# Seven products for eight in the second layer's attention, with the next sample normed twice

## The chip, the cores and the metric

The kernel runs on one core of a Trainium2 chip. The metric is the device time of one execution in microseconds, the median of several runs. A core has a matrix engine (TensorE, in the profile PE, with its weight loads as PEld), a vector engine (VectorE, DVE), an engine for functions such as the exponential (ScalarE, ACT), a general one (GpSimd, POOL), and one that issues transfers (SyncE, SP). They work side by side and wait for each other at semaphores. Each takes its own instructions in the order in which the program lists them. Results of TensorE go to PSUM, which the kernel uses in pairs of banks, a bank being 128 x 512 numbers of 32 bits; everything else stands in SBUF.

## The reference

Two attention blocks follow each other on 8 samples of 512 channels x 1024 positions, all in float32. Layer 0 has 8 heads, layer 1 has one head over all 512 channels. The change is in layer 1 and in what stands just before and after it.

```python
# layer 1; x is what layer 0 gave
n = (x - mean) * rsqrt(var + EPS) * gn_gamma + gn_beta      # mean and var of the whole sample
nf = n.reshape(b, c, h * w)                                 # c = 512, h * w = 1024
q = einsum('oc,bcs->bos', wq, nf) + bq
k = einsum('oc,bcs->bos', wk, nf) + bk
v = einsum('oc,bcs->bos', wv, nf) + bv
attn = softmax(einsum('bci,bcj->bij', q, k) * c ** (-0.5), axis=-1)
out = einsum('bcj,bij->bci', v, attn)
out = einsum('oc,bcs->bos', wo, out) + bo
return x + out
```

The kernel multiplies wq with wk, and wv with wo, once at its start. So a sample's keys in layer 1 are the normed input itself (`hs`), and the values already carry the output projection.

## The kernel before: the parts that the change touches

A product of two 2 x 2 block matrices takes eight block products, or seven with some sums and differences ahead of and behind them (one step of Strassen's recursion, in Winograd's form). The kernel already makes q, k, v and the projections this way:

```python
def strassen(multiply, done, name):          # A: blocks A11.. and S1..S4; B: blocks B11.. and T1..T4
    ...
    p1, p2 = two("o", 0, ("A11", "B11"), ("A12", "B21"))   # a pair of PSUM banks of tag "o"
    u1 = tile_u(f"u1_{name}")
    nc.scalar.copy(u1, p1)
    done(0, 0, p2, u1)
    yield                                                  # step 0
    o = banks("s", f"ps_{name}_1")                         # a pair of tag "s"
    p5, p6 = o[:, 0, :], o[:, 1, :]
    multiply(p5, "S1", "T1")
    yield                                                  # step 1
    multiply(p6, "S2", "T2")
    u2 = plus(p6, u1, "u2")                                # plus: one tensor_tensor on VectorE
    u4 = plus(p5, u2, "u4")
    yield                                                  # step 2
    p7, p4 = two("o", 2, ("S3", "T3"), ("A22", "T4"))
    u3 = plus(p7, u2, "u3")
    done(1, 1, p5, u3)
    done(1, 0, p4, u3)
    yield                                                  # step 3
    p3, _ = two("s", 3, ("S4", "B22"))
    done(0, 1, p3, u4)
    yield                                                  # step 4
```

`in_turn` runs such groups one after the other, `together` takes a step of each in turn, and `at_steps(groups, {n: [hook]})` writes other instructions into the program after step n. PSUM has two pairs of banks for each of the tags "s" and "o". The pool `t` holds 34 tiles of 128 x 1024, the pool `u` 5 of 128 x 512. The order on TensorE, VectorE and ScalarE is that of the Python text.

Layer 1's attention works on halves g of the queries, with plain products:

```python
def attention1(xs, hs, bs, b):
    ...                                    # q and v by strassen, from bs (hs and its T1..T4)
    def scores(g, kt2):                    # 2 x 128 keys x 512 queries
        s = banks("s", f"s_{name}")
        for j in range(2):
            kt = 2 * kt2 + j
            for cc in range(NC):           # NC = 4 chunks of 128 channels
                nc.tensor.matmul(s[:, j, :], piece(hs, cc, kt // 4)[...], qs[cc][:, g, :],
                                 start=cc == 0, stop=cc == NC - 1)
        ...
        p = exponentials(s, C**-0.5, accs.get(g), first, name)  # ACT: Exp of 128 x 1024; DVE: acc += p

    def values(g, ps):
        for oc2 in range(NC // 2):
            o = banks("o", f"ps_o_1_{b}_{oc2}_{g}")
            for j in range(2):
                oc = 2 * oc2 + j
                for kt in range(NT):       # NT = 8 tiles of 128 keys
                    nc.tensor.matmul(o[:, j, :], vs[kt][:, oc * P : (oc + 1) * P], ps[kt // 2][:, kt % 2, :], ...)
                if oc == 0:
                    t = banks("o", f"ps_sum_1_{b}_{g}")[:, 0, :]
                    for i in range(2):     # the sum of the exponentials over all keys
                        nc.tensor.matmul(t, ones, accs[g][:, i, :], start=i == 0, stop=i == 1)
                    inv = one_over(t, f"1_{b}_{g}")
                    held(inv, f"inv_1_{b}_{g}")
            for j in range(2):
                ...
                nc.vector.tensor_tensor(t, o[:, j, :], inv, ALU.mult)
                nc.vector.scalar_tensor_tensor(x, t, made["bias1"][:, oc : oc + 1], x, ALU.add, ALU.add)

    ps0 = [scores(0, kt2) for kt2 in range(NT // 2)]
    ps1 = [scores(1, 0)]
    values(0, ps0)
    ps1 += [scores(1, kt2) for kt2 in range(1, NT // 2)]
    values(1, ps1)
```

`one_over` lets ScalarE read the sums (`held`, for a check of their size) and then takes their reciprocal on VectorE. What surrounds it:

```python
# layer0(b): the second half of q and k of sample b; meanwhile sample b + 1 is normed, and its T1..T4 are made
hooks = {8: [lambda: score(0), lambda: score(1)]}         # first scores of layer 0
...
hooks[3] = [lambda: norm_next().normed(norm_next().xs)]
hooks[5] = [lambda: combine.first(norm_next().xs)]
hooks[7] = [combine.second]
...
at_steps(in_turn(*pairs_qk(w, 1, bs, qs, ks, b)), hooks)

# the loop over samples, after layer 0 of sample b: the first half of q and k of sample b + 1,
# from the 4 tiles of its normed x and its 4 tiles T1..T4, which are then kept for layer 0 of b + 1
at_steps(
    in_turn(*pairs_qk(next_weight(), 0, bs, qs, ks, b + 1)),
    {n + 1: [step] for n, step in enumerate(steps)},      # mean, variance, normed, T1 T2, T3 T4 of layer 1
)
...
attention1(xs, hs, combine.parts, b)
```

Of the kernel before, what the change touches and what calls it, by code (L numbers as in the profile page):

```python
# [31 lines left out]
FP = mybir.dt.float32  # L32
AF = mybir.ActivationFunctionType
ALU = mybir.AluOpType
# [6 lines left out]
P = 128  # L41
# [18 lines left out]
def two_attention_blocks(  # L60
# [32 lines left out]
    def tile2(name):  # L93
        return tpool.tile([P, 2, HALF], FP, tag="t", name=name)
# [241 lines left out]
    class Combined:  # L336


        def __init__(self, name):
            self.parts = {f"T{i}": tile2(f"t{i}_{name}") for i in range(1, 5)}  # L340

        def first(self, quarters):
            (b11, b12), (b21, b22) = quarters
            self.parts.update(B11=b11, B21=b21, B22=b22)
            nc.vector.tensor_tensor(self.parts["T1"], b12, b11, ALU.subtract)  # L345
            nc.vector.tensor_tensor(self.parts["T2"], b22, self.parts["T1"], ALU.subtract)
            self.b12 = b12
# [9 lines left out]
        c.second()  # L357
        return c.parts

    def strassen(multiply, done, name):  # L360

        def two(tag, n, *parts):
            o = banks(tag, f"ps_{name}_{n}")
            for i, (a, b) in enumerate(parts):
                multiply(o[:, i, :], a, b)
            return o[:, 0, :], o[:, 1, :]

        def plus(bank, u, what):
            t = tile_u(f"{what}_{name}")
            nc.vector.tensor_tensor(t, bank, u, ALU.add)  # L373
            return t

        p1, p2 = two("o", 0, ("A11", "B11"), ("A12", "B21"))
# [3 lines that stand above are left out]
        yield  # L380
        o = banks("s", f"ps_{name}_1")
        p5, p6 = o[:, 0, :], o[:, 1, :]
        multiply(p5, "S1", "T1")
        yield
        multiply(p6, "S2", "T2")
        u2 = plus(p6, u1, "u2")
        u4 = plus(p5, u2, "u4")
        yield
        p7, p4 = two("o", 2, ("S3", "T3"), ("A22", "T4"))
        u3 = plus(p7, u2, "u3")  # L390
        done(1, 1, p5, u3)
        done(1, 0, p4, u3)
        yield
        p3, _ = two("s", 3, ("S4", "B22"))
        done(0, 1, p3, u4)
        yield

# [14 lines left out]
    def at_steps(steps, hooks):  # L412

        n = -1
        for n, _ in enumerate(steps):
            for hook in hooks.get(n, []):
                hook()
        assert n >= max(hooks, default=-1)

    def by_channels(w, c, bs):  # L420


        def multiply(bank, a, b):
            for k in range(2):
                nc.tensor.matmul(  # L425
                    bank, w[a][:, k, c * P : (c + 1) * P], bs[b][:, k, :],
                    start=k == 0, stop=k == 1,
                )

        return multiply  # L430
# [12 lines left out]

        return multiply

    def make_channels(w, c, oc, bs, bias, to, name):

        def done(i, half, bank, u):  # L450
            n = oc + 2 * i
            nc.vector.scalar_tensor_tensor(  # L452
                to(n, half), bank, bias[:, n : n + 1], u, ALU.add, ALU.add
            )

        return strassen(by_channels(w, c, bs), done, f"{name}_{oc}")

    def make_v(w, n2, bs, vs, name):

# [75 lines left out]
    def blank(n, name):  # L535
        return [tile2(f"{name}_{i}") for i in range(n)]
# [3 lines left out]

    def pairs_qk(w, oc, bs, qs, ks, b):

        for ts, n, bias, name in [(qs, 0, V_BQ0, "q"), (ks, 1, V_BK0, "k")]:
            for i in (oc, oc + 2):
                ts[i] = tile2(f"{name}_0_{b}_{i}")
            yield make_channels(
                w.parts[n], 0, oc, bs, vec[:, bias : bias + NC],
                lambda chunk, half, ts=ts: ts[chunk][:, half, :], f"{name}_0_{b}",
            )

    ORDER = [0, 2, 1, 3]
# [1 line left out]
    def layer0(bs, qs, ks, b, load_next, norm_next):  # L553
# [72 lines left out]
        def score(i):  # L626
            ps[i] = scores(*units[i])

        w = next_weight()
        if b == 0:  # L630
            w.finish()
            waiting[0].finish()
            made["bias0"] = bias_through(square_of_parts(waiting[0]), V_BV0, V_BP0, "bias0")
        hooks = {8: [lambda: score(0), lambda: score(1)]}
        if norm_next is not None:
            hooks[0] = [lambda: norm_next().mean_of_all()]
            hooks[2] = [lambda: norm_next().variance_of_all()]
# [63 lines left out]
            held(invs.pop(at), f"inv_0_{b}_{at[0]}_{at[1]}")  # L701
        return xs, norm, bs_next

    def attention1(xs, hs, bs, b):

        qs = blank(NC, f"q_1_{b}")
        w = next_weight().parts[0]
        at_steps(in_turn(*[
            make_channels(
                w, c, c, bs, made["bias_q1"], lambda chunk, half: qs[chunk][:, half, :], f"q_1_{b}"  # L710
            )
            for c in range(2)
        ]), {})
        vs = blank(NT // 2, f"v_1_{b}")
        w = next_weight().parts[0]
        at_steps(in_turn(*[make_v(w, n2, bs, vs, f"v_1_{b}") for n2 in range(2)]), {})
        vs = [vs[nt // 2][:, nt % 2, :] for nt in range(NT)]
        accs = {}

        def scores(g, kt2):  # L720
            name = f"1_{b}_{g}_{kt2}"
            s = banks("s", f"s_{name}")
            for j in range(2):
                kt = 2 * kt2 + j
                for cc in range(NC):
                    nc.tensor.matmul(  # L726
                        s[:, j, :], piece(hs, cc, kt // 4)[:, kt % 4 * P : (kt % 4 + 1) * P],
                        qs[cc][:, g, :], start=cc == 0, stop=cc == NC - 1,
                    )
            if kt2 == 1:  # L730
                first, accs[g] = accs[g], accpool.tile(
                    [P, 2, HALF], FP, tag="acc", name=f"acc_{name}"
                )
            else:
                first = accs.get(g)
            p = exponentials(s, C**-0.5, accs.get(g), first, name)
            if kt2 == 0:
                accs[g] = p
            return p

        def values(g, ps):
            for oc2 in range(NC // 2):
                o = banks("o", f"ps_o_1_{b}_{oc2}_{g}")
                for j in range(2):
                    oc = 2 * oc2 + j
                    for kt in range(NT):
                        nc.tensor.matmul(  # L747
                            o[:, j, :], vs[kt][:, oc * P : (oc + 1) * P], ps[kt // 2][:, kt % 2, :],
                            start=kt == 0, stop=kt == NT - 1,
                        )  # L750
                    if oc == 0:
                        t = banks("o", f"ps_sum_1_{b}_{g}")[:, 0, :]
                        for i in range(2):
                            nc.tensor.matmul(t, ones, accs[g][:, i, :], start=i == 0, stop=i == 1)  # L754
                        inv = one_over(t, f"1_{b}_{g}")
                        held(inv, f"inv_1_{b}_{g}")
                for j in range(2):
                    oc = 2 * oc2 + j
                    t, x = tile_u(f"o_1_{b}_{oc}_{g}"), piece(xs, oc, g)
                    nc.vector.tensor_tensor(t, o[:, j, :], inv, ALU.mult)  # L760
                    nc.vector.scalar_tensor_tensor(
                        x, t, made["bias1"][:, oc : oc + 1], x, ALU.add, ALU.add
                    )

        ps0 = [scores(0, kt2) for kt2 in range(NT // 2)]
        ps1 = [scores(1, 0)]
        values(0, ps0)
        ps1 += [scores(1, kt2) for kt2 in range(1, NT // 2)]
        values(1, ps1)

    made = {}

# [1 line left out]
    with tc.manual_schedule(engines={PE, ACT, DVE}):  # L774
# [15 lines left out]
        for b in range(B):  # L790
            ahead = []

            def load_next():
                ahead.append(norm0(load_x(b + 1, nc.sync), b + 1))

            norm_next = (lambda: ahead[0]) if b + 1 < B else None
            xs, norm, bs = layer0(bs, qs, ks, b, load_next, norm_next)

            qs, ks = [None] * NC, [None] * NC
            hs, combine = quarters_of(f"h_1_{b}"), Combined(f"1_{b}")  # L800
            steps = [
                norm.mean_of_all, norm.variance_of_all, lambda: norm.normed(hs),
                lambda: combine.first(hs), combine.second,
            ]
            if b + 1 < B:
                at_steps(
                    in_turn(*pairs_qk(next_weight(), 0, bs, qs, ks, b + 1)),
                    {n + 1: [step] for n, step in enumerate(steps)},
                )
            else:  # L810
                for step in steps:
                    step()
            attention1(xs, hs, combine.parts, b)
            for half in range(2):
                for i in range(2):
                    nc.sync.dma_start(quarter_of(out, b, i, half), xs[i][half])
# [404 lines left out]
```

## Time and profile before

| | |
|---|---|
| median of 3 runs | 3153.16 us (3148.82 to 3154.3) |
| span of the profiled execution | 3153.6 us, mean granted TensorE clock 0.994 |
| from the scores of sample 1 to those of sample 2 in layer 1 | 745.81 to 1128.76 us, so 382.95 us a sample |
| layer 1's scores and values of sample 1 | 745.81 to 859.19 us, 113.4 us |
| HBM traffic | 48 GB/s over the span |

A line of instruction groups gives the source line, engine, operation, tiles written and read, shapes and number, then busy time, the mean ns of one, and the idle time ahead of it with what ended it. A float32 matmul leaves two records on PE, so the counts of matmuls there are twice those of the program. The end of a PE record is modelled and laps over the next, so the time of a matmul is read from the distance between starts. A timeline line gives the start, the length, and the merged instructions from there on.

### The profile page before, as it was taken

The page shows a single profiled execution, that of the slowest core. Times are in us where ns is not written, and L with a number is a line of the kernel's source. Part 1 is how long each engine was busy: PE and PEld are TensorE (multiplying, and loading weights), DVE is VectorE, ACT ScalarE, POOL GpSimd, SP SyncE. Part 2 cuts the span into 40 slices and gives each one's busy share as a digit, 9 for nine tenths or more (in the row PEclk, how much of TensorE's full clock was granted, in tenths as well). Part 3 has the DMA queues.
Part 4 walks back from the last instruction along what each step waited for, and adds up shares of the span by engine and source line. Part 5 has one row for each costly group of instructions (what it writes and reads, how often), then busy time and mean ns, then how long its engine had stood idle before and what let it go on. Part 6 is the DMA issues. An engine that isn't in the chain of part 4 may idle for free.

```text
span 3153.6 us, 33267 instructions
## 1 busy us (share of the span) xinstructions
PE 3091.7 (98%) x14370; PEld 1435.4 (46%) x14370; DVE 1808.9 (57%) x2130; ACT 835.8 (27%) x1125; POOL 13.9 (0%) x26
## 2 busy tenths in 40 slices
PE   7999999999999999999999999999999999999898
PEld 4533545335443455334553354533545335453353
DVE  4588226882278723786237852489425883248822
ACT  0162002620036100460005500154011630116200
POOL 0000000000000000000000000000000000000000
PEclk9999999999999999999999999999999999999999
DMA  6300112011120111201011011100211001020000
GB/s 230 144 1 24 70 47 81 1 47 47 54 74 1 47 47 54 74 1 70 30 70 51 1 70 63 64 24 11 83 40 64 24 24 70 14 87 1 1 0 28
DMA packets 42314, 152.70 MB, mean 48 GB/s; under 512 B 2992, under 2 KB 9136, under 8 KB 35760
## 3 DMA queue, kind: packets, MB, share of 16 engines
q1 hardware_dynamic: 38208, 146.29, 12.9%
q10 hardware_dynamic: 3952, 4.22, 0.4%
q8 instruction: 114, 1.87, 0.2%
q14 instruction: 40, 0.33, 0.0%
HBM read 122.71 MB, written 27.79 MB: 48 GB/s over the span
## 4 chain that ended last, share of the span: by engine, by line
PE 93%; DVE 6%; issue 1%; DMA 0%; ACT 0%; POOL 0%; DVEq 0%; POOLq 0%; ACTq 0%
PE s L726 14%; PE ps_o L747 14%; PE s L581 14%; PE ps_o L602 14%; PE ps_v L439 12%; PE ps_q L425 11%; PE ps_k L425 5%; PE ps_p L425 4%; PE ps_sum L616 2%; DVE p L684 1%; DVE x L687 1%; PE ps_sum L754 1%; DVE part L287 1%; PE ps_wvo L507 1%; DVE u_k L373 0%
## 5 line engine op out<-in xcount | busy, mean ns | idle before, releaser
L518 ACT ACTIVATE p<-s 128x1024 f32<-128x1024 f32 x576 | 590.3, 1025 | 922.8 <-PE s L726 581.3
L520 DVE TENSOR_TENSOR acc<-acc,p 128x1024 f32<-128x1024 f32 x416 | 508.9, 1223 | 269.0 <-ACT p L518 255.3
L581 PE MATMUL s<-q,k 64*64 64x512 f32 x4096 | 535.6, 593 | 7.2 <-DVE k L452 7.2
L602 PE MATMUL ps_o<-p,v 64*64 64x512 f32 x4096 | 528.7, 589 | 0.0
L747 PE MATMUL ps_o<-p,v 128*128 128x512 f32 x1024 | 444.7, 592 | 0.0
L726 PE MATMUL s<-q,h 128*128 128x512 f32 x1024 | 442.7, 593 | 0.0
L532 DVE RECIPROCAL inv<-ps_sum 128x512 f32<-128x512 f32 x80 | 268.4, 3356 | 183.8 <-ACT held_sum L527 183.8
L747 PEld LDWEIGHTS ps_o<-p,v 128*128 128x128 f32 x1024 | 194.6, 190 | 244.9 <-issue 244.9
L726 PEld LDWEIGHTS s<-q,h 128*128 128x128 f32 x1024 | 193.9, 190 | 243.1 <-issue 243.1
L581 PEld LDWEIGHTS s<-q,k 64*64 64x64 f32 x4096 | 148.8, 133 | 310.5 <-issue 223.6
L602 PEld LDWEIGHTS ps_o<-p,v 64*64 64x64 f32 x4096 | 156.6, 133 | 282.8 <-issue 270.9
L520 DVE TENSOR_TENSOR acc<-p,p 128x1024 f32<-128x1024 f32 x80 | 98.0, 1225 | 195.7 <-ACT p L518 195.7
L760 DVE TENSOR_TENSOR o<-ps_o,inv 128x512 f32<-128x512 f32 x64 | 44.0, 687 | 218.0 <-PE ps_o L747 218.0
L378 ACT COPY u_v<-ps_v 128x512 f32<-128x512 f32 x32 | 18.8, 586 | 421.4 <-PE ps_v L439 421.4
L373 DVE TENSOR_TENSOR u_v<-ps_v,u_v 128x512 f32<-128x512 f32 x96 | 66.3, 691 | 110.0 <-PE ps_v L439 108.9
L378 ACT COPY u_q<-ps_q 128x512 f32<-128x512 f32 x32 | 18.8, 586 | 415.2 <-PE ps_q L425 415.2
L466 DVE TENSOR_TENSOR v<-ps_v,u_v 128x512 f32<-128x512 f32 x128 | 82.8, 684 | 79.7 <-ACT u_v L378 78.6
L373 DVE TENSOR_TENSOR u_q<-ps_q,u_q 128x512 f32<-128x512 f32 x96 | 66.4, 692 | 95.5 <-PE ps_q L425 94.4
L425 PE MATMUL ps_q<-t,w_qk 128*128 128x512 f32 x256 | 118.0, 602 | 2.1 <-DVE t L345 2.1
L439 PE MATMUL ps_v<-w_v,t 128*128 128x256 f32 x512 | 113.1, 379 | 0.0
L439 PE MATMUL ps_v<-w_wvo,t 128*128 128x256 f32 x512 | 113.1, 379 | 0.0
L425 PE MATMUL ps_q<-t,w_wqk 128*128 128x512 f32 x256 | 112.5, 592 | 0.0
(138 smaller groups left out, 2628.1 us busy)
## 6 DMA issues: line engine op xcount, KB each, us to landing
x<-in_x SPq DMA_DIRECT2D x60, 512.0 KB, 8.7
w_qk<-stored_qk SPq DMA_DIRECT2D x14, 1792.0 KB, 7.3
out<-x SPq DMA_DIRECT2D x32, 512.0 KB, 2.8
w_wqk<-stored_wqk SPq DMA_DIRECT2D x8, 1792.0 KB, 7.2
w_wvo<-stored_wvo SPq DMA_DIRECT2D x8, 1792.0 KB, 7.3
w_v<-stored_v SPq DMA_DIRECT2D x7, 1792.0 KB, 7.2
w_p<-stored_p SPq DMA_DIRECT2D x7, 1792.0 KB, 7.2
stored_qk<-w_qk SPq DMA_DIRECT2D x2, 1792.0 KB, 7.1
```

Source lines behind the costliest of these rows:

```text
L373: nc.vector.tensor_tensor(t, bank, u, ALU.add)
L425: nc.tensor.matmul(bank, w[a][:, k, c * P : (c + 1) * P], bs[b][:, k, :], start=k == 0, stop=k == 1,)
L439: nc.tensor.matmul(bank[:, u * 2 * P : (u + 1) * 2 * P], bs[b][:, k, n * P : (n + 1) * P], w[a][:, k, :], start=k == 0, stop=k == 1,)
L466: nc.vector.tensor_tensor(v, pairs(bank), pairs(u), ALU.add)
L518: nc.scalar.activation(p, s, AF.Exp, scale=factor)
L520: nc.vector.tensor_tensor(acc, first, p, ALU.add)
L532: nc.vector.reciprocal(inv, ps)
L581: nc.tensor.matmul(s[cols, j, :], flat(ks[pair])[rows, k0 : k0 + HD], qs[pair][rows, g, :], start=True, stop=True,)
L602: nc.tensor.matmul(o[cols, half, :], vs[kt][rows, c0 : c0 + HD], p[rows, j, :], start=kt == 0, stop=kt == NT - 1,)
L616: nc.tensor.matmul(ps[j * HD : (j + 1) * HD, :], ones[:, :HD], accs[pair, g][:, j, :], start=True, stop=True,)
L726: nc.tensor.matmul(s[:, j, :], piece(hs, cc, kt // 4)[:, kt % 4 * P : (kt % 4 + 1) * P], qs[cc][:, g, :], start=cc == 0, stop=cc == NC - 1,)
L747: nc.tensor.matmul(o[:, j, :], vs[kt][:, oc * P : (oc + 1) * P], ps[kt // 2][:, kt % 2, :], start=kt == 0, stop=kt == NT - 1,)
```

## The change

In layer 1 the scores and the product with V also become block products of seven. The queries' quarters get S1 to S4 (`finish_q`), and the normed input already has T1 to T4, from the making of q and v. For the product with V the sums are made of the values (S1 to S4) and of the exponentials (T1 to T4), since a block product of exponentials needs differences of whole blocks. All scores of a sample therefore come first. The softmax's sums of all queries are then taken with two matmuls where there were four. Keeping all exponentials and their differences needs more of the 34 tiles; to free them, the next sample's normed input and T1 to T4 are thrown away after their use for half of q and k. While the values are computed, x is loaded again, normed again with the scale and shift that are still there, and combined again. Three smaller things move: the last product of layer 0's k goes to an "o" pair of banks, the second score of layer 0 stands behind it, and layer 1's mean and the steps after it stand one step later.

```diff
-            self.parts = {f"T{i}": tile2(f"t{i}_{name}") for i in range(1, 5)}
+            self.name, self.parts = name, {}
         def first(self, quarters):
             (b11, b12), (b21, b22) = quarters
+            for i in range(1, 5):
+                self.parts[f"T{i}"] = tile2(f"t{i}_{self.name}")
...
-        p3, _ = two("s", 3, ("S4", "B22"))
+        p3, _ = two(last, 3, ("S4", "B22"))          # last is "o" for k of oc = 1, else "s"
...
-        hooks = {8: [lambda: score(0), lambda: score(1)]}
+        hooks = {8: [lambda: score(0)], 9: [lambda: score(1)]}
...
+        def finish_q():
+            for i in range(1, 5):
+                q_parts[f"S{i}"] = tile2(f"s{i}_q_{b}")
+            finish(q_parts, a21)
+        at_steps(in_turn(*[make_v(w, n2, bs, vs, f"v_1_{b}") for n2 in range(2)]), {1: [finish_q]})
...
+        def scores(t):
+            def multiply(bank, a, b):
+                for k in range(2):
                     nc.tensor.matmul(
+                        bank, bs[b][:, k, t * P : (t + 1) * P], q_parts[a][:, k, :],
+                        start=k == 0, stop=k == 1,
                     )
+            def done(i, j, bank, u):
+                p = ps[j][t // 2][i][:, t % 2, :]
+                nc.vector.tensor_tensor(p, bank, u, ALU.add)
+                nc.scalar.activation(p, p, AF.Exp, scale=C**-0.5)
+                if late:
+                    add_up(*late.pop())              # acc += the exponentials of one done() before
+                late.append((i, p))
+            return strassen(multiply, done, f"s_1_{b}_{t}")
+        at_steps(in_turn(*[scores(t) for t in range(NT // 2)]), {})
...
+        def finish_values(n):                        # S_n of the values, T_n of the exponentials
+            for k in range(2):
+                ...
+                nc.vector.tensor_tensor(a[f"S{n}"], x, y, op)                    # 128 x 512
+                ...
+                nc.vector.tensor_tensor(b[f"T{n}"], x, y, ALU.subtract)          # 128 x 1024
+        def sums():
+            t = banks("s", f"ps_sum_1_{b}")
+            for i in range(2):
+                nc.tensor.matmul(t[:, i, :], ones, acc[:, i, :], start=True, stop=True)
+            for i in range(2):
+                invs.append(one_over(t[:, i, :], f"1_{b}_{i}"))
+        def values(c):
+            def multiply(bank, a, b):
+                for kt in range(NT // 2):
+                    nc.tensor.matmul(bank, v_parts[kt // 2][a][...], p_parts[kt // 2][b][:, kt % 2, :], ...)
+            def done(i, j, bank, u):
+                if not invs:
+                    sums()
+                ...
+                nc.vector.tensor_tensor(t, bank, u, ALU.add)
+                nc.vector.tensor_tensor(t, t, invs[j], ALU.mult)
+                nc.vector.scalar_tensor_tensor(
+                    x, t, made["bias1"][:, chunk : chunk + 1], x, ALU.add, ALU.add
+                )
+            return strassen(multiply, done, f"o_1_{b}_{c}")
+        finish_values(1)
+        hooks = {1: [lambda: finish_values(2)], 3: [lambda: finish_values(3)], 5: [lambda: finish_values(4)]}
+        ...                                          # and at_values, below
+        at_steps(together(values(0), values(1)), hooks)
...
-                    {n + 1: [step] for n, step in enumerate(steps)},
+                    {n + 2: [step] for n, step in enumerate(steps)},
...
+                at_values = {
+                    2: [load_again], 6: [lambda: again.normed(again.xs)],
+                    8: [lambda: combine_next.first(again.xs)], 9: [combine_next.second],
+                }
+                bs = combine_next.parts
```

## The prediction

> **What bounds the kernel now.** I read the shares of the engines first, then what TensorE waited for, then the costliest groups, then one sample of layer 1 in order of time.
>
> ```profile
> PE 3091.7 (98%) x14370; PEld 1435.4 (46%) x14370; DVE 1808.9 (57%) x2130; ACT 835.8 (27%) x1125; POOL 13.9 (0%) x26
> ```
>
> PE is busy for 98% of the span, so only 62 us of 3154 are without a matmul. What TensorE waited for (us in total, times, longest):
>
> ```profile
> PE ps_m L268 <- DVE stat L290: 13.3, 8, 6.2
> PE ps_wvo L507 <- DMA wo<-in_w_o: 11.2, 1, 11.2
> PE ps_p L425 <- DVE p L684: 10.9, 8, 1.4
> PE s L581 <- DVE k L452: 7.2, 8, 1.0
> ```
>
> Each is one short wait a sample, or the start. So a matmul taken away shortens the span by its whole length, as long as what feeds and empties it keeps up. The groups concerned:
>
> ```profile
> L520 DVE TENSOR_TENSOR acc<-acc,p 128x1024 f32<-128x1024 f32 x416 | 508.9, 1223 | 269.0 <-ACT p L518 255.3
> L747 PE MATMUL ps_o<-p,v 128*128 128x512 f32 x1024 | 444.7, 592 | 0.0
> L726 PE MATMUL s<-q,h 128*128 128x512 f32 x1024 | 442.7, 593 | 0.0
> L760 DVE TENSOR_TENSOR o<-ps_o,inv 128x512 f32<-128x512 f32 x64 | 44.0, 687 | 218.0 <-PE ps_o L747 218.0
> ```
>
> Scores (L726) and values (L747) have 1024 records each, so 512 matmuls, 64 a sample; neither waits for anything. The mean of 592 ns laps over the next record. The distance between starts gives the true time (timeline of PE, sample 1):
>
> ```profile
> 745.81 34.57 PE L726 MATMUL s<-q,h 128*128 128x512 f32 x80
> 780.22 7.03 PE L747 MATMUL ps_o<-p,v 128*128 128x512 f32 x16
> 787.09 1.88 PE L754 MATMUL ps_sum<-acc,ones 128*128 128x512 f32 x4
> 788.80 20.76 PE L747 MATMUL ps_o<-p,v 128*128 128x512 f32 x48
> ```
>
> 80 records are 40 matmuls, and 780.22 - 745.81 = 34.41 us, so 0.860 us each. Four records of the sums are two matmuls in 1.71 us. The whole stretch has 132 matmuls in 113.4 us (0.859). How the other engines stood in four stretches (length, then busy us of PE, PEld, DVE, ACT, POOL, clock, DMA): scores, values with sums, v of layer 1, and the end of layer 0's projection.
>
> ```profile
> 745.90:780.40 34.50, 34.50 (x82) 15.37 (x82) 4.64 (x5) 4.10 (x4) 0.00 (x0) 1.00 0.15 54
> 780.40:809.50 29.10, 29.10 (x69) 12.84 (x69) 6.15 (x5) 2.44 (x5) 0.00 (x0) 1.00 0.05 19
> 721.70:745.90 24.20, 24.20 (x114) 21.11 (x113) 9.52 (x15) 1.17 (x2) 0.00 (x0) 1.00 0.21 76
> 1027.70:1054.80 27.10, 25.74 (x65) 10.74 (x62) 24.41 (x31) 3.17 (x7) 0.00 (x0) 1.00 0.00 1
> ```
>
> Layer 1's attention leaves VectorE nearly free. The third row is a Strassen stage made `in_turn`: TensorE has no gap. The fourth is one made `together` with VectorE 90% busy: it cost TensorE 1.36 us. These two are my models for the new scores and the new values.
>
> **What the Trainium skill says.** "FP8 and Floating Point Precision", TensorE Precision Notes: true FP32 takes 4 passes through the array. "TensorE: Matmul & The Clock Gate", What's actually happening, gives the array 2.4 GHz; an estimate from both is 4 x 512 / 2.4 = 853 ns a matmul, and the trace shows 860. So the time lies in the columns streamed, and block products of the same shape cost the same. "VectorE: DVE Perf Modes", The TRN2 errata: an fp32 tensor_tensor of N columns takes (N + 151) / 0.96 ns, so 691 and 1224; the trace has 692 (u_q) and 1223 (L520). "PSUM — Partial Sum Buffer", PSUM bank collisions: two engines may not touch one bank at once, so the program has to order them. The trace agrees: the reciprocal (L532, 3356 ns) follows ScalarE's read of the sum.
>
> **TensorE's part.** Scores: 4 groups x 7 products x 2 matmuls = 56 a sample, not 64. Values: 2 x 7 x 4 = 56, not 64. Sums: 2, not 4. That is 18 fewer, all 128 x 512: 18 x 0.861 = 15.5 us a sample, 124.0 us in 8. I count all of it, because none of the removed matmuls hid a wait.
>
> **The small moves.** The mean of layer 1 one step later: PE's wait for L290 was 13.3 us in 8, of which 6.2 in the last sample, where there is no q and k to put it behind and nothing changes. The other 7.1 us should go. First scores of layer 0: the wait of 7.2 us was for k to leave the "s" banks; with a product between the two scores and another pair of banks it should go too. At the very end, three VectorE steps follow the last product in place of four (2.8 us from 3143.47): 0.7 us, once.
>
> **VectorE in the scores.** Per sample 12 sums u, 16 sums in `done` and 14 additions to acc, 42 x 0.69 = 29.0 us, beside 56 x 0.861 = 48.2 us of TensorE. ScalarE: 16 exponentials of 128 x 512 at about 0.6 (held_inv of that shape took 625 ns) and 4 copies of 0.59, 12 us. With 60% load and the same banks as in the stage for v I expect no wait. An addition to acc stands one `done` behind its exponential, so it finds it done. The four sums of `finish_q` (4 x 1.22 = 4.9 us) fall into v's 24 us, where VectorE had 9.5: no wait.
>
> **VectorE in the values: the tight place.** `finish_values` 8 x (0.69 + 1.22) = 15.3; reciprocals 2 x 3.36 = 6.7; u 6 x 0.69 = 4.1; `done` 8 x (0.69 + 0.69 + 0.75) = 17.0; norming again 4 x 0.54 = 2.2; T1 to T4 again 4 x 1.22 = 4.9. Sum 50.2 us, beside 58 x 0.861 = 49.9 of TensorE. It is as full as the projection. So I laid both orders side by side, with 0 at the first product of values:
>
> - TensorE: p1 and p2 of the first half to 6.9, the two sums to 8.6, p1 and p2 of the second to 15.5, p5 twice to 22.4, p6 twice to 29.3, p7 and p4 of the first to 36.2, of the second to 43.0, p3 twice to 49.9.
> - VectorE: last additions to acc to 2.2, S1 and T1 to 6.0, reciprocals (first sum 7.8, ScalarE's read to 8.6) to 15.4, two `done` to 19.9, S2 and T2 to 23.7, S3 and T3 to 27.5, u2 and u4 twice to 30.8, S4 and T4 to 34.6, then u3 and two `done` of the first half to 39.5, norming to 41.7, those of the second to 46.6, the last `done` and T1 to T4 to about 56.
>
> Where they meet: T2's first half is needed at 22.4 and ready at 21.9; its second at 24.1 and 23.7; T4's first half at 32.7 and 32.7; its second at 34.5 and 34.6. So p6 just passes and p4 may wait some tenths. Later VectorE is behind, but p3 needs only the bank of p5, free at 43.1, while TensorE comes there at 46.8. The next sample's v then runs its first two products from the normed x, needs T1 at 53 (ready 50) and T4 near 59 (ready 56). I put the waits at 0.5 us a sample, 4 us in all.
>
> **The second load.** 2 MB more for seven samples, against 48 GB/s over the span. In the order of transfers these loads stand behind the store of the first quarter of x, which is ready at about 20; their tiles were set free earlier, at the end of the scores. The listing of transfers has 8.7 us from issue to landing for x, so they land near 31, and norming comes at 39.5. Hidden.
>
> **The sum.** 3153.2 - 124.0 - 7.1 - 7.2 - 0.7 + 4 = 3018 us, 4.3% less.
>
> **Rivals.** First, VectorE becomes the bound in the values. For it: 50.2 against 49.9, and a chain of sums, reciprocals and differences with no slack at p4. The projection with the same fill lost 1.36 us. Against it: independent VectorE instructions follow each other faster than their length (L661 to L662 in the projection start 0.60 us apart at 0.68 us each). If it bites, it makes 2 to 4 us a sample: 3030 to 3046. Second, the reload is late: it shares the transfers with the weights, and one store holds back four loads. Then norming holds VectorE, the banks of p5 stay taken, and p3 waits. It has some 8 us to spare before norming waits and some 3 more before TensorE does; past that it may cost 5 us a sample, near 3055. Third, a chain in the scores: bank to sum to exponential to addition through two engines, with a wait at each group; 1 us in each of 32 groups is 3046. Against it is that the same banks and the same steps leave no gap in v. Fourth, the new stages have no waits at all: 3014.
>
> **Range and chances.** The 124 us are counted work on an engine that is 98% busy; nothing in the rivals eats more than a third of them, two together perhaps half. The lower end is the count without waits and a little run-to-run spread, the upper is one rival in full: 3008 to 3042. The line for 2% faster is 3090, 72 us above my value; I give 0.95 to faster, 0.04 to the same, 0.01 to slower.
>
> **What would show it.** In the profile after: 448 matmuls (896 records) each in scores and values, 16 sums, starts 0.860 us apart for each; a sample's period 382.95 - 15.5 - 1.0 - 1.0 + 0.5 = 366 us; DVE near 2270 us busy (0.75 of the span); the waits of ps_m and of the first s gone; a wait of p4 for T4 of some tenths and none in the scores; no idle time of norming for x. It would be wrong if PE's list of waits shows several us a sample behind L789 to L819, or behind the loads, or if the granted clock falls below 0.99.

## The result and the profile after

| | before | after |
|---|---|---|
| median, measured side by side | 3152.46 us (3148.82 to 3154.3) | 3028.26 us (3026.07 to 3028.86) |
| scores and values of sample 1 in layer 1 | 113.38 us | 98.69 us (727.52 to 826.21) |
| one sample, scores to scores | 382.95 us | 367.36 us (727.52 to 1094.88) |

The ratio is 0.9606, 95% interval 0.9589 to 0.9623: 124 us less. The forecast was 3018, so 134 us or so; the value lies within the range. I read the profile after in the order of the prediction: shares of the engines first.

```profile
PE 2966.2 (98%) x14082; PEld 1379.1 (46%) x14082; DVE 2234.1 (74%) x2746; ACT 899.1 (30%) x1265; POOL 13.9 (0%) x26
```

TensorE has 125.5 us less work and is still busy for 98%: it remains the bound. VectorE has 425 us more and stays under it. What TensorE waited for (us in total, times, longest):

```profile
PE ps_wvo L509 <- DMA wo<-in_w_o: 11.2, 1, 11.2
PE ps_p L427 <- DVE p L686: 10.9, 8, 1.4
PE ps_q L427 <- DVE q L454: 10.2, 7, 1.5
PE ps_m L268 <- DVE stat L290: 6.2, 1, 6.2
PE ps_o L807 <- DVE t_p L793: 3.6, 8, 0.5
```

Three things are to be seen. The wait of the first scores for k has left the list. Of the wait for layer 1's mean (L290) only the last sample's 6.2 is left. But a line that before did not have stands third: 1.45 us in each of seven samples, ps_q behind L454. It is larger than the 1.02 us that the mean's wait was before. The last line is the tight place of the values, 0.46 a sample.

Scores (L745, four forms) and values (L807, four forms) have 896 records each, 448 matmuls. Of the two only the values stand in the list, and they wait for T2. One sample of layer 1 in two stretches, scores and then values with sums (length, busy us of PE, PEld, DVE, ACT, POOL, clock, DMA):

```profile
727.50:775.60 48.10, 48.10 (x114) 21.29 (x113) 24.73 (x39) 10.55 (x18) 0.00 (x0) 1.00 0.11 38
775.60:826.20 50.60, 50.14 (x117) 21.70 (x116) 43.96 (x55) 8.94 (x17) 0.00 (x0) 1.00 0.20 68
```

56 matmuls in 48.07 us are 0.858 each: the scores run without a gap, VectorE half busy beside them. 58 in 50.62 us are 0.74 us more than 58 x 0.860 = 49.88. Where in the values that is lost, the timeline of PE tells:

```profile
775.59 7.03 PE L807 MATMUL ps_o<-p,v 128*128 128x512 f32 x16
782.45 1.88 PE L800 MATMUL ps_sum<-acc,ones 128*128 128x512 f32 x4
784.17 7.03 PE L807 MATMUL ps_o<-p,v 128*128 128x512 f32 x16
791.03 7.03 PE L807 MATMUL ps_o<-t_p,s_v 128*128 128x512 f32 x16
798.52 10.59 PE L807 MATMUL ps_o<-t_p,s_v 128*128 128x512 f32 x24 [0.46 <-DVE t_p L793]
```

p6 starts at 798.52, 22.9 after the first product and not at 22.4 or so; the profile shows no wait for p4, p7 and p3 behind it. T2 was late because the reciprocals were. On VectorE (start, length, what ended the idle time; the last line is the norming again):

```profile
785.09 3.36 DVE L534 RECIPROCAL inv<-ps_sum 128x512 f32<-128x512 f32 x1 [2.34 <-ACT held_sum L529]
789.20 3.36 DVE L534 RECIPROCAL inv<-ps_sum 128x512 f32<-128x512 f32 x1 [0.75 <-ACT held_sum L529]
...
817.76 1.91 DVE L328 TENSOR_SCALAR x<-x,scale,shift 128x512 f32<-128x512 f32 x4
```

and on ScalarE, which reads each sum ahead of its reciprocal:

```profile
784.37 0.60 ACT L529 ACTIVATE held_sum<-ps_sum 128x512 f32<-128x512 f32 x1 [1.13 <-PE ps_sum L800]
...
788.48 0.60 ACT L529 ACTIVATE held_sum<-ps_sum 128x512 f32<-128x512 f32 x1 [3.42 <-DVE inv L534]
```

ScalarE's first read comes only when both sums are made, and its second waits 3.42 us until the first reciprocal is through, although it reads the other bank. So the second reciprocal starts 0.75 us late and ends 17.0 us after the first product; the forecast had 15.4.

The new wait stands in the first half of the next sample's q and k, where the mean was moved (timeline of PE):

```profile
1027.45 0.28 PE L268 MATMUL ps_m<-stat,in_sample 128*128 128x4 f32 x2
1027.59 3.68 PE L427 MATMUL ps_q<-t,w_qk 128*128 128x512 f32 x8
1031.11 0.28 PE L268 MATMUL ps_v<-spread,in_sample 128*128 128x4 f32 x2
1032.84 1.98 PE L427 MATMUL ps_q<-x,w_qk 128*128 128x512 f32 x4 [1.45 <-DVE q L454]
```

The mean (ps_m) is ready now. But the variance (ps_v), which follows it by a step, stands right ahead of p3 of q, and both want a pair of "s". p3 waits for L454, the reader of p5: it was given p5's pair. That pair is free only after p7 and p4 have ended, u3 has been made from p7, and p5 has been read. In the kernel before, TensorE had waited a little earlier, for the mean:

```profile
1061.08 0.39 PE L268 MATMUL ps_m<-stat,in_sample 128*128 128x4 f32 x2 [1.02 <-DVE stat L290]
```

Each wait in these lists is somewhat smaller than what the starts say was lost. p3 of q starts 1.73 us after the variance's product (1031.11 to 1032.84) and not the 0.14 that this product takes from start to start without a wait (1063.12 to 1063.26 before), so 1.59 are lost and 1.45 listed. p6 starts 7.49 us after p5 (791.03 to 798.52) and not the 6.86 that the eight matmuls before them take, so 0.63 are lost and 0.46 listed. For the mean before it is 1.19 for 1.02 (2.91 us from 1058.17 to 1061.08, for two matmuls that take 1.72).

### The profile page after: what moved, and what is told of

Same layout as the page of the kernel before. It is cut to its first block, busy times and chain, and to the rows that moved or that the text cites. A ratio compares the mean times of both kernels' runs of the same rounds, so it can differ in the third digit from the quotient of the medians.

```text
span 3027.1 us, 33513 instructions
## 1 busy us (share of the span) xinstructions
PE 2966.2 (98%) x14082; PEld 1379.1 (46%) x14082; DVE 2234.1 (74%) x2746; ACT 899.1 (30%) x1265; POOL 13.9 (0%) x26
## 4 chain that ended last, share of the span: by engine, by line
PE 93%; DVE 6%; issue 0%; ACT 0%; DMA 0%; POOL 0%; POOLq 0%; DVEq 0%
PE s L583 15%; PE ps_o L604 15%; PE ps_q L427 13%; PE ps_v L441 13%; PE ps_s L745 13%; PE ps_o L807 9%; PE ps_k L427 6%; PE ps_p L427 5%; PE ps_sum L618 2%; DVE inv L534 2%; DVE p L686 1%; PE ps_wvo L509 1%; DVE x L819 0%; DVE x L689 0%; DVE o L818 0%; PE ps_sum L800 0%
## 5 line engine op out<-in xcount | busy, mean ns | idle before, releaser
L520 ACT ACTIVATE p<-s 128x1024 f32<-128x1024 f32 x512 | 523.5, 1024 | 333.6 <-PE s L583 329.6
L807 PE MATMUL ps_o<-t_p,s_v 128*128 128x512 f32 x384 | 169.7, 595 | 3.6 <-DVE t_p L793 3.6
L745 PE MATMUL ps_s<-s_q,t 128*128 128x512 f32 x384 | 170.0, 592 | 0.0
L753 ACT ACTIVATE p<-p 128x512 f32<-128x512 f32 x128 | 80.1, 630 | 253.0 <-DVE p L752 253.0
L375 DVE TENSOR_TENSOR u_s<-ps_s,u_s 128x512 f32<-128x512 f32 x96 | 66.4, 692 | 117.6 <-PE ps_s L745 116.5
L752 DVE TENSOR_TENSOR p<-ps_s,u_s 128x512 f32<-128x512 f32 x128 | 86.6, 687 | 68.6 <-ACT u_s L380 67.6
L807 PEld LDWEIGHTS ps_o<-t_p,s_v 128*128 128x128 f32 x384 | 71.6, 190 | 99.1 <-issue 82.0
L745 PE MATMUL ps_s<-q,h 128*128 128x512 f32 x256 | 115.1, 592 | 0.0
L745 PEld LDWEIGHTS ps_s<-s_q,t 128*128 128x128 f32 x384 | 73.0, 190 | 91.8 <-issue 88.0
L807 PE MATMUL ps_o<-p,v 128*128 128x512 f32 x256 | 112.5, 592 | 0.0
```

What stands on the lines that cost most here:

```text
L520: nc.scalar.activation(p, s, AF.Exp, scale=factor)
L745: nc.tensor.matmul(bank, bs[b][:, k, t * P : (t + 1) * P], q_parts[a][:, k, :], start=k == 0, stop=k == 1,)
L752: nc.vector.tensor_tensor(p, bank, u, ALU.add)
L807: nc.tensor.matmul(bank, v_parts[kt // 2][a][:, kt % 2, c * P : (c + 1) * P], p_parts[kt // 2][b][:, kt % 2, :], start=kt == 0, stop=kt == ...
```

## The experiments

They ask four things: what the moved mean is worth, what the tight place in the values is worth and what makes it, whether norming again is really hidden, and whether two idle-looking stages have the room they seem to have. "A" in the expectations is my reading of the two traces, the "rival" is named in each.

**The changed kernel again**, beside the next three on one chip, as their measure.

> The changed kernel once more, as it is, for comparison with the next three on the same chip. Every theory: within 3 us of its 3028.3.

Measured: 3025.93 us (3024.53 to 3029.51), ratio 0.9603 (0.9590 to 0.9616). The runs from "T2 ahead of the values" on are on other chips. They are set against this time too, since the kernel before took 3150.8 to 3152.4 us beside each of them.

**The mean back at its old step.**

```diff
-                    {n + 2: [step] for n, step in enumerate(steps)},
+                    {n + 1: [step] for n, step in enumerate(steps)},
```

> The changed kernel with layer 1's mean and the steps after it back where they stood before. Theory A (moving them took away a wait of 1.02 us of TensorE for the mean's statistics and put one of 1.45 us of a product for the bank of p5 in its place): 7 x 0.43 = 3 us shorter, 3025, with the wait of ps_m back at 13 us in all and that of ps_q for L454 gone. Rival, the move itself works as I predicted and the shortfall lies elsewhere: 7 us longer, 3035.

Measured: 3026.64 us, ratio 0.9602 (0.9589 to 0.9615). The wait for L290 is 13.3 us in 8 again and the one for L454 is gone, so one wait did take the other's place. The small gain of 3 us that I expected isn't resolved by the time: the two intervals lie on each other. That the move brings 7 us is excluded.

**The mean moved, but the variance and what follows it behind p3.**

```diff
-                    {n + 2: [step] for n, step in enumerate(steps)},
+                    {n: [step] for n, step in zip((2, 4, 5, 6, 7), steps)},
```

> The mean stays one step later, the variance's matmul goes behind p3 of q, and the steps after it one later still. Theory A: neither the wait of 1.02 nor that of 1.45 us is left, so 7 x 1.45 = 10 us shorter than the changed kernel, 3018. Rival B (VectorE is so full there that the time is only given back at another wait): 3026 to 3030, with a new wait of the products of k or of layer 1's q.

Measured: 3016.74 us, ratio 0.9577 (0.9563 to 0.9590), 9.2 us below the changed kernel beside it. The same stretch of PE's timeline:

```profile
1021.62 0.28 PE L268 MATMUL ps_m<-stat,in_sample 128*128 128x4 f32 x2
1021.76 3.68 PE L427 MATMUL ps_q<-t,w_qk 128*128 128x512 f32 x8
1025.27 1.88 PE L427 MATMUL ps_q<-x,w_qk 128*128 128x512 f32 x4
1027.01 0.39 PE L268 MATMUL ps_v<-spread,in_sample 128*128 128x4 f32 x2
```

p3 of q now stands ahead of ps_v and starts without a gap. So the wait came from the variance's place; the steps that follow it moved too, but use no banks. q and k's first half takes 24.60 us here (1014.75 to 1039.35), 25.77 with the mean at its old step: 1.17 us less in each of seven samples, 8.2 us, where the times of the two runs differ by 9.9. The idea of moving the mean was worth its 7 us once the variance was kept away from p3.

**The small moves alone, on the kernel before.** Layer 1's attention stays with eight products; only the k, the second score and the mean are moved.

```diff
-        p3, _ = two("s", 3, ("S4", "B22"))
+        p3, _ = two(last, 3, ("S4", "B22"))
-        hooks = {8: [lambda: score(0), lambda: score(1)]}
+        hooks = {8: [lambda: score(0)], 9: [lambda: score(1)]}
-                    {n + 1: [step] for n, step in enumerate(steps)},
+                    {n + 2: [step] for n, step in enumerate(steps)},
```

> The kernel before with only the small moves: k's last product to the other banks, the second score behind it, the mean and its steps one step later; no block product is added or taken away. The prediction as it stands on record: 7.1 + 7.2 = 14 us shorter than before, 3138. Theory A: about 8 x 1.18 for k, from the two traces, less 7 x 0.43 for the mean, so 6 us shorter, 3146.

Measured: 3143.88 us against 3151.1, ratio 0.9978 (0.9970 to 0.9987): 7.2 us less and not 14. Among PE's waits the line stands here too, with the old line numbers, so seven products have no part in it:

```profile
PE ps_q L425 <- DVE q L452: 10.2, 7, 1.5
```

**T2 ahead of the values.** S2 and T2 are made right behind S1 and T1, before the reciprocals.

```diff
         finish_values(1)
-        hooks = {1: [lambda: finish_values(2)], 3: [lambda: finish_values(3)], 5: [lambda: finish_values(4)]}
+        finish_values(2)
+        hooks = {3: [lambda: finish_values(3)], 5: [lambda: finish_values(4)]}
```

> S2 and T2 of the values and exponentials are made right behind S1 and T1, ahead of the reciprocals. Theory A (the 0.46 us that p6 waits for T2 and the small losses near it are a matter of order, not of VectorE's load): 0.5 to 0.8 us a sample, 4 to 6 us shorter than the changed kernel, 3023, with no wait of PE for L793. Rival B (VectorE's 50 us of work beside 50 of TensorE is the limit): the wait moves to T4, 3026 to 3030.

Measured: 3020.52 us, ratio 0.9585 (0.9571 to 0.9598). The values' five products from p5 to p7 are one stretch in PE's timeline, and the stage takes 49.88 us (773.58 to 823.46), the bare 58 x 0.860:

```profile
789.03 17.33 PE L807 MATMUL ps_o<-t_p,s_v 128*128 128x512 f32 x40
```

**One subtraction of T2 made twice**, 1.2 us more of VectorE a sample at the tight place.

```diff
                 nc.vector.tensor_tensor(b[f"T{n}"], x, y, ALU.subtract)
+                if (n, k) == (2, 0):
+                    nc.vector.tensor_tensor(b[f"T{n}"], x, y, ALU.subtract)
```

> One subtraction more, the first half of T2 a second time: 1.22 us of VectorE a sample, at the place where p6 waits. Theory A: no slack there, so the whole 1.1 to 1.2 us a sample, 9 to 10 us longer, 3038; PE's wait for L793 grows from 0.46 to about 1.6 us a sample. Rival (slack that my reading of the trace misses): 3028.

Measured: 3036.0 us, ratio 0.9640 (0.9625 to 0.9654), 10 us above the changed kernel. p6's wait grew from 0.46 to 1.72 us, by the 1.26 us between the starts of the two subtractions (793.62 to 794.88):

```profile
796.16 10.59 PE L809 MATMUL ps_o<-t_p,s_v 128*128 128x512 f32 x24 [1.72 <-DVE t_p L795]
```

So here VectorE's time goes into the kernel's time one for one (1.26 us x 8 = 10.1).

**The two sums in two pairs of banks.** Nothing else is changed.

```diff
-            t = banks("s", f"ps_sum_1_{b}")
+            ts = [banks("s", f"ps_sum_1_{b}_{i}")[:, 0, :] for i in range(2)]
             for i in range(2):
-                nc.tensor.matmul(t[:, i, :], ones, acc[:, i, :], start=True, stop=True)
+                nc.tensor.matmul(ts[i], ones, acc[:, i, :], start=True, stop=True)
             for i in range(2):
-                invs.append(one_over(t[:, i, :], f"1_{b}_{i}"))
+                invs.append(one_over(ts[i], f"1_{b}_{i}"))
```

> The changed kernel with the two sums in two pairs of banks in place of two banks of one pair; S2 and T2 stay where they are. In the changed kernel ScalarE's read of the second sum waits 3.42 us for the first reciprocal, because both lie in one pair, and the second reciprocal starts 0.75 us late; the first read also waits for both sums. Theory A (this, not the load of VectorE, is why T2 comes late): the reciprocals follow each other without a gap and end 1.4 us earlier, PE's wait for L793 is gone, 4 to 6 us shorter than the changed kernel, about 3021. Rival: the reads wait for something else or T4 is then late, 3025 to 3029.

Measured: 3020.86 us, ratio 0.9584 (0.9571 to 0.9597), as much as from T2 ahead. ScalarE reads the second sum 0.92 us after the first, and the reciprocals follow each other (ScalarE, then VectorE):

```profile
783.11 0.60 ACT L529 ACTIVATE held_sum<-ps_sum 128x512 f32<-128x512 f32 x1 [0.27 <-PE ps_sum L800]
...
784.03 0.60 ACT L529 ACTIVATE held_sum<-ps_sum 128x512 f32<-128x512 f32 x1 [0.23 <-PE ps_sum L800]
```

```profile
783.83 6.57 DVE L534 RECIPROCAL inv<-ps_sum 128x512 f32<-128x512 f32 x2 [1.48 <-ACT held_sum L529]
```

The reciprocals end at 790.40, 15.2 us after the first product at 775.19, where the forecast had 15.4. p6 no longer waits.

**Without norming again.** The second load stays; its norming and the four combinations are left out, and the next sample's second products take the raw x and its quarters, so the output is another one. 7.1 us of VectorE and 3.2 of ScalarE a sample are left out.

```diff
-                    2: [load_again], 6: [lambda: again.normed(again.xs)],
-                    8: [lambda: combine_next.first(again.xs)], 9: [combine_next.second],
+                    2: [load_again, lambda: raw()],       # B11.. and T1..T4 become quarters of the raw x
                 }
-                bs = combine_next.parts
+                bs = {}
```

> x of the next sample is loaded again but neither normed nor combined again: layer 0's v and half of its q and k then use x as loaded and its own quarters in place of T1 to T4, so the work left out is 7.1 us of VectorE and 3.2 of ScalarE a sample, and the output is another one. Theory A (hidden work): within 3 us of 3028, at most 1 us a sample less. Rival B (VectorE bounds the product with V): 2 to 4 us a sample less, 3000 to 3014.

Measured: 3026.95 us, ratio 0.9608 (0.9593 to 0.9622): no difference, and the same waits on PE. Norming again costs nothing. The load itself stays in this run, so of its cost only the traces tell.

**The queries' sums made twice**, 4.9 us more of VectorE a sample while v is made, a stage in which it had nearly 10 us to spare.

```diff
             finish(q_parts, a21)
+            finish(q_parts, a21)
```

> The four sums S1 to S4 of q a second time: 4.9 us more of VectorE a sample, in the making of v. Theory A: hidden, within 3 us of 3028, because VectorE has 10 us of room in that stage. Rival B (VectorE's share of the span as such costs time): 2 to 5 us a sample, 3044 or more.

Measured: 3038.93 us, ratio 0.9647 (0.9633 to 0.9662). This expectation was missed by 11 us. In place of no wait, p5 of v's second group waits (PE's timeline):

```profile
717.67 7.14 PE L441 MATMUL ps_v<-w_wvo,t 128*128 128x256 f32 x32 [1.43 <-DVE v L468]
```

VectorE shows why: all eight sums stand in one block ahead of v's own steps.

```profile
713.66 1.22 DVE L175 TENSOR_TENSOR s_q<-q,s_q 128x1024 f32<-128x1024 f32 x1
714.79 2.01 DVE L375 TENSOR_TENSOR u_v<-ps_v,u_v 128x512 f32<-128x512 f32 x3
716.84 2.48 DVE L468 TENSOR_TENSOR v<-ps_v,u_v 128x512 f32<-128x512 f32 x4
```

The block lasts from 705.47 to 714.79. Only then come u2, u4, u3 and the sum that reads p5, and TensorE wants p5's banks for the next group before that. By the starts p5 comes 1.60 us later than in the changed kernel (6.77 us from 710.90 to 717.67 in place of 5.17), 12.8 us in 8, which is nearly all of the 13.0 above the changed kernel. So from the four added sums, 4 x 1.14 = 4.6 us, 1.6 arrived, and the room at this step is some 3 us, not the stage's 10.

**The scores alone by seven**, the values with eight products and two sums.

> Only the scores by seven block products, as in the changed kernel, with its small moves and the next sample normed twice; the product with V plain again, 64 matmuls, with two matmuls of sums. Theory A: 8 + 2 matmuls fewer a sample than before, 10 x 0.860 x 8 = 69 us, and 6 us from the moves, so 3077, and no wait of TensorE in the scores. Rival (the chain bank, sum, exponential, addition costs 1 us a group): 3085 to 3105.

Measured: 3072.93 us against 3150.81, ratio 0.9752 (0.9738 to 0.9767). No line of the scores or of the values is among PE's waits. The 77.9 us less are 10 matmuls x 0.861 x 8 = 68.9 and the small moves' 7.2, to within 2 us.

**Both orders**: the variance behind p3 and T2 ahead, the two edits above together.

> The changed kernel with the variance's matmul behind p3 and with S2 and T2 ahead of the reciprocals, e3 and e5 in one. Theory A: the two gains add, 10 and 4 to 6 us, so 3013. Rival B: less than the larger of the two, 3018 to 3028.

Measured: 3009.03 us (3008.74 to 3012.15), ratio 0.9552 (0.9538 to 0.9565). The two gains add up: 16.9 us less than the changed kernel, where the single runs gave 9.2 and 5.4. A sample's period is 365.12 us, 2.24 below the changed kernel's; q and k's first half gives 1.50 of it (26.10 to 24.60), the values 0.74. This is the best version of the study, ahead of the kernel before and of the changed one.

## Why the prediction was right, and where it was off

- **Eighteen matmuls fewer, each worth its whole length: right.** 14.69 us a sample, 117.5 in 8, where 124.0 less 4 were forecast. In the run with the scores alone their 56 products again take 48.07 us (728.85 to 776.92), 0.858 each.
- **No wait in the scores, none in v: right, but for v by a reason that does not hold.** Nothing of L745 or of v is in the list. I had set the 4.9 us of `finish_q` against VectorE's idle time in the whole stage. The queries' sums made twice show that the room was some 3 us behind the sums, so that it sufficed was partly luck.
- **"I put the waits at 0.5 us a sample" in the values: right in place and kind, mis-sized.** The stage lost 0.74, 5.9 us in 8; 0.46 of each shows as p6's wait; 0.17 more lies between the same two starts, and about 0.1 further on, without a wait beside it. All of it goes when T2 is early. The term that was off is "reciprocals (first sum 7.8, ScalarE's read to 8.6) to 15.4": it is 17.0, since the two sums share one pair of banks. I had each bank waited for by itself; with the sums in two pairs the 15.4 comes true. p6 and not p4 therefore bears the wait.
- **u3 behind p7: wrong in time, harmless in the values.** It was laid at 34.6 and started at 37.1 (812.67), at the end of p4 and not of p7: p7 and p4 lie in one pair. In the values p3 had enough room for it. In the moved mean it had not.
- **k's last product in the "o" banks: right, undersized.** Forecast 7.2 us. From layer 0's first score to the first product of q, 906.22 to 1054.74 before and 873.24 to 1020.58 after, it is 1.18 us a sample, 9.4 in 8. The 7.2 were the listed waits, and here too the starts say more: before, the second score came 2.03 us after the first, which takes 0.86, so 1.17 were lost.

```profile
908.25 1.09 PE L581 MATMUL s<-q,k 64*64 64x512 f32 x8 [0.95 <-DVE k L452]
```

- **"The other 7.1 us should go": the step that failed.** The removed wait did go, but I counted only it. The variance is moved by the same edit, and stands where p3 needs its banks. q and k's first half took 25.77 us before and takes 26.10 after: 0.33 us more in each of seven samples, 2.3 us lost in place of 7.1 won. That a wait could take the place of the one removed is not among my rivals: I had looked for new waits in the new stages alone.
- **The second load is hidden: right.** Loads were issued 21.6 us after the first product and had landed by 31; VectorE's norming came at 42.2 (817.76), behind its own queue and not behind the load.
- **The end: 0.7 forecast, 0.6 measured** (10.3 us from the last product to the end before, 9.7 after).

The sum by the traces: 3152.5 - 117.5 - 9.4 + 2.3 - 0.6 = 3027.3, against 3028.3 measured. Of the 10 us by which the forecast was low, the moved mean is 9.4 (7.1 + 2.3), the values are 2.5 (120.0 - 117.5), and k gives 2.2 back.

What stays open: why the listed waits are 0.14 to 0.22 us smaller than the losses between starts. The projection's wait of 1.36 us a sample, which no part of the change touches, is in all runs and wasn't tried.

## What to carry to other kernels

Where one engine is busy for 98%, count what is taken from it at its measured distance between starts, waits too, and spend the rest of the effort on deadlines: for each hand-over of a bank, when the last reader is done and when the next writer comes. A step that is moved takes the ones behind it along, so each of them has to be laid against the banks at its new place, not only the one whose wait is to be removed. And the idle time of a stage is no measure of its room: a block of added work counts against the next hand-over behind it.

## What the runs showed that I had not expected

- Two results in one pair of banks are waited for together. ScalarE's read of one bank waited 3.42 us for VectorE's reciprocal of the other; in two pairs it didn't wait for that. The Trainium skill's "PSUM — Partial Sum Buffer", PSUM bank collisions, asks for order within one bank only. In both runs the two sums lie in different banks and only the pair differs, so I take this order for the program's, which follows the pair as a whole; no run tests two banks of one pair without it.
- Independent sums on VectorE start closer than they are long: 1.14 us apart at 1.22 us each for 1024 columns (the block of eight), 0.61 apart at 0.68 for an S of 512 columns with a T behind it (796.64 to 797.25). A VectorE laid out by lengths is a little too full: 2234 us busy where I had about 2270.
- A block of 4.6 us on an engine with 10 us idle in the same stage cost 1.6 us of the kernel's time, eight times.
